# A patch-match network on one core: the first image is loaded over two queues ahead of the weights, and its first strips are gathered chunk by chunk

## The chip, the cores and the metric

The kernel runs on one core of one Trainium2 chip. The metric is the device time of one execution in microseconds (us), lower is better. The number compared is the median of several executions of the same program.

Engines, as the profile calls them: PE (matrix multiply; PEld is its weight load), DVE (vector), ACT (scalar/activation), POOL (GpSimd) and SP (SyncE, which here only issues DMAs). ACT and POOL issue DMAs too. Each engine takes its own instructions strictly in program order, so an instruction that waits holds back everything queued behind it on that engine.

## The reference

Eight images x[b] of 32 channels and 128 x 128 pixels go through two layers, each with a residual. Cut to what matters:

```python
n = group_norm(x)                                   # 16 groups
cost[o] = box3x3(sum_c (n - shift(n, o))**2)        # 25 offsets o of a 5x5 window
idx     = the 8 offsets with the lowest cost        # for every pixel
xb      = the 8 shifted copies of n picked by idx   # 32 * 8 = 256 channels
h = relu(dw2(w1 @ xb)); h = relu(dw4(w3 @ h))       # 1x1, then depthwise 3x3
wiener  = sigmoid(dw6(w5 @ h))
x = x + agg_w @ (inv_dct * (wiener * dct(xb)))
x = x + conv5x5(group_norm(x))                      # layer 1, one 5x5 kernel
```

## The kernel before

**Preparation of an image** (`prep`, L342). The image is loaded as `xn` with the four groups of 32 rows on the four quarters of the partitions (`load_image`, L78: one large DMA per quarter at L85, and six single edge rows at L90). Statistics (`bn_stats`, L349), a small matmul chain (`group_stats`, L254) and one scaling instruction (L360) normalise it. Then:

- `sources` (L375) transposes the rows and stores them to DRAM (`xl`, then `xtd`): 32 DMAs at L387 and 18 at L395/L399, all issued by POOL.
- `squares` (L403) forms the differences `df` on DVE (L414), their squares on ACT (L422), and the sum over channels on PE (L429, into `pd`). There are six groups of rows i = 0 to 5, with 12 differences each. `df` has four buffers, so DVE cannot write a fifth difference before PE has read the first. A finished group is copied (`sm`, L440) and stored to `sq` by POOL.
- After groups 1, 3, 4 and 5, `costs` (L455) of **chunk** 0, 1, 2 and 3 can run. A chunk is a quarter of the places: 8 of the 32 rows of every row group. 13 DMAs by POOL (L462, L469) bring the costs into `dsum`, DVE adds the 3 x 3 neighbours (`v`, L478 to L490, about four instructions), PE transposes (`pt`, L495), ACT copies (`ct`, L499), and DVE searches the eight best (L506, L507: 16 pairs for each half of a chunk).
- `places` (L512) turns a chunk's offsets into table places (`o`, L520 to L529, on DVE), PE transposes them, ACT casts them (`li`, L540), POOL stores them to DRAM (`idxd`, L541). Only then is the chunk marked `ready`.

**Gather** (units). An image has 16 strips of 8 rows; a strip has four units. `gather_load` (L552) has POOL load source pixels `xt` (three buffers) and two index tiles `ib` per unit by a DMA from `idxd` (L574; five buffers). `gather_select` (L582) makes a one-hot tile from each of them on ACT (L588, then L589). `gather_pixels` (L592) multiplies (`pg`, L603, PE) and ACT copies the result to `xb` (L610). Strip n needs chunk n % 4: strips 0 to 3 need one more chunk each, and from strip 4 on all chunks of that image are there.

**The three stages** of a strip, i = 1, 2, 3: `pointwise_v` (PE `pv` L641, ACT copy to `tv` L649), `pointwise_t` (PE `p` L665, ACT copy to `t` L672, and DMAs by SP), `depthwise_v` (ACT L692, then eight DVE multiply-adds `acc` at L695, ACT L699) and `depthwise_t` (PE `pw` L718, ACT L731). At the end `final_load`, `final_dct` (`pc` L777, DVE L785) and `final_add` (`pa` L798, DVE L805).

**The order** is written out by hand in the loop at L942: step s runs stage i on strip s - (i - 1) for i = 3, 2, 1 and then the final part, and in each of these four quarters it places one unit's gather: select of unit u + 1, load of unit u + 3, pixels of unit u. Preparation is made of generators in four queues ("D" with costs in us, "A", "P", "Q"); `tick` (L911) runs as much of "D" as is owed per quarter, and `until` (L918) runs the queues until a condition holds. `unit` (L892) calls `until` in front of a `gather_load` whose chunk is not yet `ready`, so that everything emitted later on PE, DVE and ACT stands behind that chunk's work. In `run` (L223) the first entry of "D" that is due is taken, except that at most two pairs of differences (cost `PAIR`) go between two runs of "Q".

Ahead of the loop, L932 loads units 0 to 6, selects up to unit 4 and gathers up to unit 3. As units 4 to 6 belong to strip 1, chunks 0 and 1 are both finished in front of strip 0's first stage, and the loads of the loop, three units ahead, ask for chunks 2 and 3 in the same way.

```python
        for u in range(7):
            unit(gather_load, u)
            unit(gather_select, u - 2)
            unit(gather_pixels, u - 3)
        u = 4
```

**Start.** The whole first image is issued by ACT (L95). SP meanwhile issues the constants `cst` (L97), the depthwise weights `dwv` and `dwt` (L123, L154), the pointwise weights (L174), 32 small DMAs `dq` (L284) and the rest. In the block at L148 the pointwise weights are reordered on DVE (`w_kc`, L179), transposed on PE (L189) and copied by ACT (L190); POOL builds `dwd` (L162) from `dwt`. `mixes` (L276) builds `ldct` and `lagg`.

Of the kernel before, what the change touches and what calls it, by code (L numbers as in the profile page):

```python
# [16 lines left out]
P = 128  # L17
C, K, H, W = 32, 8, 128, 128
CK = C * K
# [24 lines left out]
def bm3d_conv_preact(  # L44
# [30 lines left out]
        tc.tile_pool(name="ps_d", bufs=1, space=bass.MemoryType.PSUM)  # L75
    )

    def load_image(b, engine):  # L78

        xn = xnp.tile([P, HR, HX], F32, name=f"xn_{b}", tag="xn")  # L80
        for rg in range(4):
            s = slice(C * rg, C * (rg + 1))
            lo = 32 * rg - 3
            a, z = max(lo, 0), min(lo + HR, H)
            engine.dma_start(xn[s, a - lo : z - lo, 2 : 2 + W], x[b, :, a:z, :])  # L85
            for r in range(HR):
                y = lo + r
                if y < 0 or y >= H:
                    y = min(max(y, 0), H - 1)
                    engine.dma_start(  # L90
                        xn[s, r : r + 1, 2 : 2 + W], x[b, :, y : y + 1, :]
                    )
        return xn

    first = load_image(0, nc.scalar)  # L95
    cst = const.tile([P, C_N], F32, name="cst")
    nc.sync.dma_start(cst, consts)  # L97
    ident = cst[:, C_ID : C_ID + P]
# [46 lines left out]
    nc.vector.tensor_scalar(inner, inner, -1.0, 1.0, op0=ALU.mult, op1=ALU.add)  # L145


    with tc.tile_pool(name="setup", bufs=1) as sp, tc.tile_pool(  # L148
        name="setup_ps", bufs=2, space=bass.MemoryType.PSUM
    ) as spp:  # L150
        dwt = sp.tile([P, 3, 4, 9], F32, name="dwt")
        for n, w in enumerate((w2, w4, w6)):
            for g in range(4):
                nc.sync.dma_start(  # L154
                    dwt[C * g : C * (g + 1), n],
                    w[:P].rearrange("(q c) o a b -> c q (o a b)", c=C),
                )
            nc.gpsimd.memset(dwd[0:C, n, 1], 0.0)
            for u in range(2):
                for dy in range(3):  # L160
                    s = slice(C * (u + dy), C * (u + dy + 1))
                    nc.gpsimd.tensor_tensor(  # L162
                        dwd[s, n, u],
                        cst[s, C_M32 : C_M32 + C]
                        .unsqueeze(1)
                        .unsqueeze(1)
                        .to_broadcast([C, 4, 3, C]),
                        dwt[s, n, :, 3 * dy : 3 * dy + 3].unsqueeze(3).to_broadcast([C, 4, 3, C]),
                        ALU.mult,
                    )  # L170
        wide = {}
        for name, w in (("w1", w1), ("w3", w3), ("w5", w5)):
            t = sp.tile([P, 2, CK], F32, name=f"nat_{name}", tag=f"nat_{name}")
            nc.sync.dma_start(t, w.rearrange("(m p) i a b -> p m (i a b)", p=P))  # L174
            if name == "w1":

                nat, t = t, sp.tile([P, 2, CK], F32, name="w1_kc")
                for m in range(2):
                    nc.vector.tensor_copy(  # L179
                        t[:, m].rearrange("p (k c) -> p k c", c=C),  # L180
                        nat[:, m].rearrange("p (c k) -> p k c", k=K),
                    )
            wide[name] = t
        for name, dst in (("w1", lw1), ("w3", lw3), ("w5", lw5)):
            for g in range(2):
                ps = spp.tile([P, CK], F32, name=f"ps_{name}_{g}", tag="ps")
                for m in range(2):
                    src = wide[name][:, m, g * P : (g + 1) * P]
                    nc.tensor.transpose(ps[:, m * P : (m + 1) * P], src, ident)  # L189
                nc.scalar.copy(dst[:, g], ps)  # L190

    xbp = ctx.enter_context(tc.tile_pool(name="xb", bufs=2))
    accp = ctx.enter_context(tc.tile_pool(name="acc", bufs=1))
# [29 lines left out]
    def run(which, credit=1e9):  # L223

        q, took = queues[which], 0.0
        for _ in range(len(q) if which != "D" else 1000):

            i = next(
                (
                    i  # L230
                    for i, (c, _, at) in enumerate(q)
                    if at <= now[0] and (c != PAIR or pairs[0] < 2)
                ),
                None,
            )
            if i is None or took >= credit:
                break
            cost, task, _ = q[i]
            del q[i]
            took += cost  # L240
            pairs[0] += cost == PAIR
            push(task)
        if which == "Q":
            pairs[0] = 0
        return took
# [8 lines left out]
    def group_stats(mv, name):  # L254
# [18 lines left out]
        yield from inverse_std(mr[:, 1:2], tmp[:, 0:1], tmp[:, 0:1])  # L273
        return mr

    def mixes():  # L276

        dq = work.tile([P, 2, K], F32, name="dq", tag="dq", bufs=1)
        src = dct_w.rearrange("(m h c i) k a b -> m h k c (i a b)", m=2, h=2, i=K)
        for k in range(K):  # L280
            for m in range(2):
                for h in range(2):
                    p = 64 * h + 8 * k
                    nc.sync.dma_start(dq[p : p + 8, m], src[m, (h + m + 1) % 2, k])  # L284
        m8 = work.tile([P, 8], F32, name="m8", tag="m16", bufs=1)
        yield "D", 1.0
        nc.vector.tensor_reduce(
            m8,
            cst[:, C_M32 : C_M32 + C].rearrange("p (a c) -> p c a", c=8),
            axis=mybir.AxisListType.X,  # L290
            op=ALU.add,
        )
        for m in range(2):
            nc.vector.tensor_tensor(
                ldct[:, m].rearrange("p (c i) -> p c i", i=K),
                m8.unsqueeze(2).to_broadcast([P, 8, K]),
                dq[:, m].unsqueeze(1).to_broadcast([P, 8, K]),
                ALU.mult,
            )

        iv = work.tile([P, 2, K], F32, name="iv", tag="iv", bufs=1)
        nc.sync.dma_start(iv, inv_w.rearrange("(m p) k a b -> p m (k a b)", p=P))
        ag = work.tile([C, CK], F32, name="ag", tag="xr")
        nc.sync.dma_start(ag, agg_w.rearrange("c i a b -> c (i a b)"))
        for m in range(2):
            yield "D", 0.5
            ib = work.tile([P, P], F32, name=f"ib_{m}", tag="xm")
            nc.vector.tensor_tensor(
                ib.rearrange("p (c k) -> p c k", k=K),
                cst[:, C_M16 : C_M16 + 16].unsqueeze(2).to_broadcast([P, 16, K]),  # L310
                iv[:, m].unsqueeze(1).to_broadcast([P, 16, K]),
                ALU.mult,
            )
            yield "P", 0
            ps = ps_x.tile([P, 512], F32, name=f"ps_ag_{m}", tag="x")[:, :C]
            nc.tensor.transpose(ps, ag[:, m * P : (m + 1) * P], ident[:C, :C])
            agt = work.tile([P, C], F32, name=f"agt_{m}", tag="agt")
            nc.scalar.copy(agt, ps)
            yield "P", 0
            ps2 = ps_x.tile([P, 512], F32, name=f"ps_ia_{m}", tag="x")[:, :C]  # L320
            nc.tensor.matmul(ps2, ib, agt, start=True, stop=True)
            nc.scalar.copy(lagg[:, m], ps2)
# [602 lines left out]

    with tc.manual_schedule(engines=ORDERED):
        push(prep(0))
        push(mixes())
        xbd[0] = dram.tile([P, 2, H, W], F32, name="xbd_0", tag="xbd")
        for i in range(3):  # L930
            nc.gpsimd.memset(tb[i][0:64, :, 0], 0.0)
        for u in range(7):  # L932
            unit(gather_load, u)
            unit(gather_select, u - 2)
            unit(gather_pixels, u - 3)
        u = 4

        dt = dv = kept = iter(())

# [2 lines left out]
        for s in range(len(steps) + 2):  # L942
            if s < len(steps):
                b, n = steps[s]
                if s == 2:
                    push(bands())
                if n == (0 if b else 4) and b + 1 < NB:
                    until(lambda: b in ready, 4.0)
                    push(prep(b + 1))
                if n == NS - 1 and b + 1 < NB:  # L950
                    until(lambda: b + 1 in ready, 4.0)
                    xbd[b + 1] = dram.tile([P, 2, H, W], F32, name=f"xbd_{b+1}", tag="xbd")
            for i in (3, 2, 1, 0):
                si = s - (i - 1 if i else 2)
                live = 0 <= si < len(steps)
# [18 lines left out]
                    final_dct(bi, ni, accs[3, bi, ni], xf, j0, j1)  # L974

                run("Q")
                if s < len(steps):
                    unit(gather_select, u + 1, (0,))
                    unit(gather_load, u + 3)
                    tick(b, i)  # L980
                next(new_v, None)
                if live and i:
                    pointwise_t(i, bi, ni, lws[i - 1], src)
                next(kept, None)
                if s < len(steps):
                    unit(gather_pixels, u)
                next(dt, None)
                run("A")
                next(dv, None)
                if s < len(steps):  # L990
                    unit(gather_select, u + 1, (1,))
                    u += 1
                next(dt, None)
                kept, dv, dt = dv, new_v, new_t
                if live and not i:
# [68 lines left out]
```

## Time and profile before

| | us |
|---|---|
| median of 3 executions (lowest, highest) | 6942.3 (6939.84, 6943.18) |
| the profiled execution: its time, its span | 6939.75, 6938.0 |
| busy: PE, DVE, ACT, POOL | 6488.0, 5777.4, 5067.6, 3018.7 |
| first `bn_stats` of image 0 (L349) starts | 40.81 |
| first difference `df` (L414) starts | 52.85 |
| first `v` of chunk 0 (L478) starts | 95.52 |
| places of chunk 0, 1, 2, 3 ready on DVE (end of L529) | 134.49, 180.93, 229.75, 265.25 |
| step 4's first matmul (`pv`, L641, stage 3 of strip 2) starts | 382.77 |

Times inside the execution count from the start of the span. A group line of the profile gives the engine, what is written from what, how often, busy time and mean ns, then the idle time in front and what ended it. A line of the timeline gives start, length, engine, line, operation, and in brackets the idle time before it and its releaser. A line of the stretches view gives, for each engine, busy us and the number of instructions, and at its end the granted PE clock (1.00 is full), the busy share of the DMA engines and GB/s.

### The profile page before, as it was taken

The numbers are of one execution on the slowest core, as the hardware profiler recorded it, in microseconds if no ns is written. First come the engines' busy times: TensorE is split into PE (matmuls) and PEld (weight loads), VectorE is DVE, ScalarE is ACT, GpSimd is POOL, SyncE is SP. The second block draws the span as 40 slices with busy tenths as digits, with TensorE's granted clock in tenths as the row PEclk, the third lists the DMA queues.
The fourth block names the chain that finished last, engine by engine and source line by source line (L and its number), as shares of the span: only waits on it lengthen the run. The fifth ranks groups of instructions, "written<-read, shape, count | busy, mean of one in ns | idle before, by whom it ended". The sixth has DMA issues, their size and how long they took to land.

```text
span 6938.0 us, 230820 instructions
## 1 busy us (share of the span) xinstructions
PE 6488.0 (94%) x100450; PEld 3042.2 (44%) x100450; DVE 5777.4 (83%) x8606; ACT 5067.6 (73%) x6698; POOL 3018.7 (44%) x5143
## 2 busy tenths in 40 slices
PE   4699999999999999999999999999999999999997
PEld 1344444444444444444444444444444444444443
DVE  6689988889888898888988898888988889877775
ACT  4687778777687777877777776877768777776772
POOL 6345436334463344534445334553435433333332
PEclk9799999999999999999999999999999999999998
DMA  3566656557565575656756567565666666556652
GB/s 79 132 149 148 156 141 160 147 147 161 144 154 148 137 166 133 162 144 142 162 134 164 142 144 163 142 161 137 152 149 147 165 142 143 143 151 154 156 143 66
DMA packets 774196, 1007.83 MB, mean 145 GB/s; under 512 B 223712, under 2 KB 587168, under 8 KB 773184
## 3 DMA queue, kind: packets, MB, share of 16 engines
q0 software_dynamic: 387104, 733.70, 42.1%
q1 hardware_dynamic: 381056, 256.86, 17.2%
q8 instruction: 791, 12.96, 0.8%
q10 hardware_dynamic: 5024, 2.49, 0.2%
q14 instruction: 221, 1.81, 0.1%
HBM read 542.24 MB, written 217.01 MB: 109 GB/s over the span
## 4 chain that ended last, share of the span: by engine, by line
PE 48%; DVE 23%; issue 8%; DMA 8%; ACT 7%; POOL 5%; SPq 0%; POOLq 0%; DVEq 0%; ACTq 0%
PE pw L718 17%; DVE acc L695 16%; PE pv L641 12%; PE p L665 9%; PE pg L603 3%; PE p L861 3%; DMA t<-t 2%; DVE df L414 2%; PE pc L777 2%; DMA xf<-xbd 2%; DVE idx L507 2%; ACT ib L588 1%; PE pa L798 1%; ACT df L422 1%; DMA dsum<-sq 1%
## 5 line engine op out<-in xcount | busy, mean ns | idle before, releaser
L695 DVE SCALAR_TENSOR_TENSOR acc<-tv,dwv,acc 128x1024 f32<-128x1024 f32 (+3 forms) x3264 | 4031.9, 1237 | 242.1 <-ACT acc L692 126.5
L718 PE MATMUL pw<-t,dwd 96*32 96x508 f32 (+6 forms) x19392 | 2162.2, 592 | 84.7 <-DMA t<-t 58.5
L574 POOL DMA_DIRECT2D ib<-idxd x1024 | 566.7, 554 | 2185.9 <-ACT sel L589 2050.3
L718 PEld LDWEIGHTS pw<-t,dwd 96*32 96x32 f32 (+1 forms) x19392 | 712.3, 112 | 1216.7 <-issue 1135.5
L588 ACT ACTIVATE ib<-ib,nplace 128x1024 bf16<-128x1024 bf16 x1024 | 1170.6, 1143 | 19.1 <-DMA ib<-idxd 19.1
L589 ACT ACTIVATE sel<-ib 128x1024 f32<-128x1024 bf16 x1024 | 1084.5, 1059 | 32.5
L665 PE MATMUL p<-acc,lw 128*32 128x256 f32 x16768 | 981.7, 379 | 5.2 <-ACT tv L649 5.2
L641 PE MATMUL pv<-acc,lw 128*128 128x512 f32 (+1 forms) x2112 | 967.3, 601 | 16.7 <-DVE acc L785 16.0
L758 POOL DMA_DIRECT2D xf<-xbd x1088 | 648.7, 630 | 229.3 <-PE pc L777 121.3
L603 PE MATMUL pg<-sel,xt 128*32 128x48 f32 x45056 | 603.6, 209 | 151.3 <-DVE acc L785 63.7
L665 PEld LDWEIGHTS p<-acc,lw 128*32 128x32 f32 x16768 | 552.8, 111 | 427.2 <-issue 44.9
L649 ACT COPY tv<-pv 128x512 f32<-128x512 f32 (+2 forms) x784 | 438.8, 577 | 408.2 <-PE pv L641 399.4
L603 PEld LDWEIGHTS pg<-sel,xt 128*32 128x32 f32 x45056 | 586.6, 113 | 321.2 <-DVE acc L785 90.5
L422 ACT ACTIVATE df<-df 128x786 f32<-128x786 f32 (+2 forms) x576 | 468.8, 860 | 273.9 <-DVE df L414 271.1
L731 ACT ACTIVATE acc<-pw 128x512 f32<-128x512 f32 (+2 forms) x808 | 440.9, 572 | 268.6 <-PE pw L718 268.2
L641 PEld LDWEIGHTS pv<-acc,lw 128*128 128x128 f32 x2112 | 380.2, 191 | 505.7 <-issue 422.6
L672 ACT COPY t<-p 128x512 f32<-128x512 f32 x800 | 426.0, 571 | 225.1 <-PE p L665 223.0
L699 ACT ACTIVATE acc<-acc 128x1024 f32<-128x1024 f32 (+3 forms) x408 | 416.8, 1022 | 199.4 <-DVE acc L695 199.1
L805 DVE TENSOR_TENSOR xr<-xr,pa 128x256 f32<-128x256 f32 (+2 forms) x136 | 55.0, 404 | 587.3 <-PE pa L798 581.2
L414 DVE TENSOR_TENSOR df<-xn 128x786 f32<-128x786 f32 (+2 forms) x576 | 528.5, 967 | 11.4 <-PE pd L429 10.1
L692 ACT ACTIVATE acc<-tv,dwv 128x1024 f32<-128x1024 f32 (+3 forms) x408 | 454.6, 1114 | 51.7 <-PE pa L798 36.4
L641 PE MATMUL pv<-xb,lw 128*128 128x512 f32 x1024 | 474.3, 606 | 0.0
(128 smaller groups left out, 6041.6 us busy)
## 6 DMA issues: line engine op xcount, KB each, us to landing
ib<-idxd POOLq DMA_DIRECT2D x1024, 256.0 KB, 4.4
xbd<-xb POOLq DMA_DIRECT2D x128, 1024.0 KB, 6.4
xf<-xbd POOLq DMA_DIRECT2D x960, 128.0 KB, 6.6
t<-t SPq DMA_DIRECT2D x792, 128.0 KB
t<-t SPq DMA_DIRECT2D x384, 256.0 KB
tv<-tv SPq DMA_DIRECT2D x384, 130.0 KB
xt<-xtd POOLq DMA_DIRECT2D x240, 176.0 KB, 5.0
xl<-xs POOLq DMA_DIRECT2D x256, 64.0 KB, 2.3
```

Of the source, the lines that this page charges most:

```text
L414: nc.vector.tensor_sub(df[:, :, ca:cz], xn[:, r0 : r0 + SR, ca:cz], xn[:, r0 + dy : r0 + dy + SR, ca + dx : cz + dx],)
L422: nc.scalar.activation(df[:, :, ca:cz], df[:, :, ca:cz], AF.Square)
L574: nc.gpsimd.dma_start(ib.rearrange("p k y x -> p (k y x)"), idxd[b][s4 // 8, s4 % 8, 4 * k0 : 4 * k0 + 8] .rearrange("k x -> (k x)") .part ...
L588: nc.scalar.activation(ib, ib, AF.Square, bias=nplace)
L589: nc.scalar.activation(sel, ib, AF.Relu, scale=-1.0, bias=1.0)
L603: nc.tensor.matmul(pg[C * j : C * (j + 1), :, xa:xz], xt[:, t], sels[j // 2][:, j % 2, :, xa:xz], start=True, stop=True,)
L641: nc.tensor.matmul(ps[:, :hr], lhsT[:, g, P:CK], src(g)[:, h : h + hr], start=g == 0, stop=g == 1,)
L665: nc.tensor.matmul(ps[C * r : C * (r + 1), e, :nb], lhsT[:, g, s], rows[:, r : r + 4 * nb - 3 : 4], start=g == 0, stop=g == 1,)
L692: nc.scalar.activation(acc, rows, AF.Copy, scale=tap)
L695: nc.vector.scalar_tensor_tensor(acc, rows, tap, acc, op0=ALU.mult, op1=ALU.add)
L718: nc.tensor.matmul(pt[u][C * j : C * (j + 1), : nh[u], :nb, xa:xz], dwd[0:hi, i - 1, u, j, dx + 1], t[0:hi, j, : nh[u], :nb, xa + dx : xz ...
L758: nc.gpsimd.dma_start(xf[p : p + C, m, j0:j1], src[g, m, (h + m + 1) % 2, :, :, ya:yz])
```

## The change

1. `load_image` takes several engines and deals the four quarters of the image out in turn. Image 0 goes over ACT (quarters 0 and 2) and SP (quarters 1 and 3). SP issues its two quarters in front of `cst` and of all weights.
2. The load, reordering, transposing and copying of the pointwise weights leave the setup block and become a generator `weights()`, whose DVE, PE and ACT instructions are placed among the differences of image 0. Its tiles use `acc` buffers, its PSUM tiles come from the common pool. `mixes()` is due a little later too.
3. While image 0 has no chunks all ready (`0 not in ready`), `run("D")` takes any due entry that is not a pair of differences first. So the search and the places of a chunk come ahead of differences.
4. The units of strips 0 to 3 are gathered chunk by chunk: `begin(u)` loads three units and selects one, at the first unit of each chunk; `whole` places one unit complete, and nothing of the next chunk (`limit`). Strip 0's four units stand ahead of the loop. Step 0 gathers nothing. Steps 1 and 2 gather four units, two in each of their first two quarters; step 3 gathers eight, two in each quarter. From step 4 on it is one unit per quarter, as before.

The order of instructions that the changed kernel gives to PE is the same as before from its instruction row 679 on, which is step 4's first matmul, and it has the same PE instructions in all. DVE, ACT, POOL and SP, too, agree with before from about that point to the end.

```diff
-    def load_image(b, engine):
+    def load_image(b, *engines):
...
         for rg in range(4):
+            engine = engines[rg % len(engines)]
...
-    first = load_image(0, nc.scalar)
+    first = load_image(0, nc.scalar, nc.sync)
...
+            if which == "D" and 0 not in ready:
+
+                i = next((k for k, (c, _, at) in enumerate(q) if at <= now[0] and c != PAIR), i)
             if i is None or took >= credit:
...
+    def weights():
+
+        natural, kc = {}, None
+        for i, (name, w) in enumerate((("w1", w1), ("w3", w3), ("w5", w5))):
+            t = accp.tile([P, 2, R * W // 2], F32, name=f"nat_{name}", tag=f"acc{i + 1}0")
+            natural[name] = t = t[:, :, :CK]
+            nc.sync.dma_start(t, w.rearrange("(m p) i a b -> p m (i a b)", p=P))
+        yield "D", 1.0, 8
+
+        nat = natural["w1"]
+        kc = accp.tile([P, 2, R * W // 2], F32, name="w1_kc", tag="acc31")
+        natural["w1"] = kc = kc[:, :, :CK]
+        for m in range(2):
+            nc.vector.tensor_copy(
+                kc[:, m].rearrange("p (k c) -> p k c", c=C),
+                nat[:, m].rearrange("p (c k) -> p k c", k=K),
+            )
+        for name, dst in (("w1", lw1), ("w3", lw3), ("w5", lw5)):
+            for g in range(2):
+                yield "P", 0
+                ps = ps_x.tile([P, 512], F32, name=f"ps_{name}_{g}", tag="x")
+                for m in range(2):
+                    nc.tensor.transpose(
...
+                nc.scalar.copy(dst[:, g], ps[:, :CK])
...
-        yield "D", 1.0
+        yield "D", 1.0, 10
...
         push(prep(0))
+        push(weights())
         push(mixes())
...
-        for u in range(7):
-            unit(gather_load, u)
-            unit(gather_select, u - 2)
-            unit(gather_pixels, u - 3)
-        u = 4
+
+        def begin(u):
+            for k in range(3):
+                unit(gather_load, u + k)
+            unit(gather_select, u)
+
+        def whole(u, end):
+            if u + 1 < end:
+                unit(gather_select, u + 1)
+            if u + 3 < end:
+                unit(gather_load, u + 3)
+            unit(gather_pixels, u)
+            return u + 1
+
+        begin(0)
+        u = 0
+        while u < 4:
+            u = whole(u, 4)
...
+            count = {0: (0, 0, 0, 0), 1: (2, 2, 0, 0), 2: (2, 2, 0, 0), 3: (2, 2, 2, 2)}
+            count = count.get(s, (1, 1, 1, 1)) if s < len(steps) else (0, 0, 0, 0)
+            limit = 4 * (s + 1) if s < 3 else len(units)
+            if 0 < s < 4:
+                begin(u)
...
+                more = count[3 - i]
+                if more:
+                    if u + 1 < limit:
+                        unit(gather_select, u + 1, (0,))
+                    if u + 3 < limit:
+                        unit(gather_load, u + 3)
...
                     tick(b, i)
...
+                if more:
                     unit(gather_pixels, u)
...
+                if more:
+                    if u + 1 < limit:
+                        unit(gather_select, u + 1, (1,))
                     u += 1
+                    if more > 1:
+                        u = whole(u, limit)
```

More of the change, by code (lines that the diff above doesn't have):

```diff
@@ L145, in bm3d_conv_preact @@
     nc.vector.tensor_scalar(inner, inner, -1.0, 1.0, op0=ALU.mult, op1=ALU.add)
-    with tc.tile_pool(name="setup", bufs=1) as sp, tc.tile_pool(
-        name="setup_ps", bufs=2, space=bass.MemoryType.PSUM
-    ) as spp:
+    with tc.tile_pool(name="setup", bufs=1) as sp:
         dwt = sp.tile([P, 3, 4, 9], F32, name="dwt")
@@ L170, in bm3d_conv_preact @@
                     )
[L171 to L190, printed above, removed]
     xbp = ctx.enter_context(tc.tile_pool(name="xb", bufs=2))
@@ L274, in group_stats @@
         return mr
+    def weights():
[19 more added lines that the diff above has]
+                    nc.tensor.transpose(
+                        ps[:, m * P : (m + 1) * P],
+                        natural[name][:, m, g * P : (g + 1) * P],
+                        ident,
+                    )
+                nc.scalar.copy(dst[:, g], ps[:, :CK])
     def mixes():
@@ L976, in bm3d_conv_preact @@
                 run("Q")
+                more = count[3 - i]
[4 more added lines that the diff above has]
+                        unit(gather_load, u + 3)
                 if s < len(steps):
-                    unit(gather_select, u + 1, (0,))
-                    unit(gather_load, u + 3)
                     tick(b, i)
@@ L984, in bm3d_conv_preact @@
                 next(kept, None)
-                if s < len(steps):
+                if more:
                     unit(gather_pixels, u)
@@ L989, in bm3d_conv_preact @@
                 next(dv, None)
-                if s < len(steps):
-                    unit(gather_select, u + 1, (1,))
+                if more:
+                    if u + 1 < limit:
+                        unit(gather_select, u + 1, (1,))
                     u += 1
+                    if more > 1:
+                        u = whole(u, limit)
                 next(dt, None)
```

## The prediction

> **What bounds the kernel now.** I read the stretches view first, over the start of the execution, then the chain of waits, then the timeline of ACT and DVE. In the stretches the columns are PE, PEld, DVE, ACT, POOL, then PE clock, DMA share, GB/s.
>
> ```profile
> 52.85:95.50 42.65, 36.13 (x192) 9.85 (x192) 35.98 (x40) 36.21 (x51) 35.33 (x52) 1.00 0.34 64
> 95.50:134.50 39.00, 19.07 (x88) 4.34 (x88) 37.58 (x129) 18.48 (x24) 30.79 (x42) 0.82 0.46 100
> 134.50:181.00 46.50, 15.82 (x147) 5.24 (x147) 30.51 (x119) 20.62 (x26) 22.92 (x41) 0.72 0.28 75
> 181.00:230.00 49.00, 11.43 (x363) 9.71 (x364) 19.98 (x108) 22.14 (x26) 18.88 (x31) 0.53 0.44 111
> 340.00:382.80 42.80, 42.65 (x744) 20.30 (x742) 33.78 (x30) 34.08 (x43) 14.14 (x26) 1.00 0.66 149
> ```
>
> PE is full only from about 300 us on (42.65 of 42.80 us in the last row). Before that the start is held by DVE (37.58 of 39.00) or by nobody: from 134 to 230 us every engine is under two thirds. The page's 94% for PE says nothing of this stretch, and the change touches no other: from step 4's first matmul (382.77 us) all orders are the old ones. So the change is worth what it does to the time of that matmul. The chain of waits and DMA view show why the start begins late:
>
> ```profile
> 0.75 6.09 DMA xn<-in_x_dram
> 11.48 6.87 DMA xn<-in_x_dram
> 19.79 5.71 DMA dq<-in_L_conv_dct_w_dram
> 30.50 5.38 DMA dq<-in_L_conv_dct_w_dram
> 40.90 4.76 DVE st L349 x8
> ...
> q10 hardware_dynamic: 5024, 2.49, 22.3%
> ```
>
> The image's quarters alternate with SP's small DMAs. The last line (first 60 us; ACT's queue) says that the image itself needs 22.3% of 60 us, 13.4 us. The timeline shows the round trip of a chunk:
>
> ```profile
> 137.08 0.41 ACT L540 CAST li<-pi 128x128 bf16<-128x128 f32 x2
> 146.65 1.15 ACT L588 ACTIVATE ib<-ib,nplace 128x1024 bf16<-128x1024 bf16 x1 [9.16 <-DMA ib<-idxd]
> 201.42 1.15 ACT L588 ACTIVATE ib<-ib,nplace 128x1024 bf16<-128x1024 bf16 x1 [9.97 <-DMA ib<-idxd]
> 213.54 0.20 DVE L506 MAX8 mx<-ct 128x8 f32<-128x25 f32 x1 [25.25 <-ACT ct L499]
> ```
>
> From ACT's `li` over the store, the load and the landing of `ib` ACT stands still for 9 us, and DVE then waits for `ct` or squares that stand behind the selects in ACT's queue: 25.25 us here, 13.17 at 156.17. DVE's idle gaps from 95.5 to 382.8 add up to about 70 us.
>
> **The change, leg by leg.** F is the start of the first difference, before 52.85.
>
> *Leg 1, image.* `bn_stats` to first difference took 52.85 - 40.81 = 12.05 and stays. Two image queues bound the landing between 13.4 + 2 (first packets at about 2) = 15 and four quarters in turn at 6.1 to 6.9 plus edges, 28. No row shows two large loads side by side. `cst` now stands behind SP's half; it took 3.2 (0.76 to 3.98), and DVE needs it after two `bn_stats`: +1 to +3. F lies in 28 (15 + 12 + 1) to 43 (28 + 12 + 3); I take 31 (17 + 12 + 2), nearer the low end, as one queue fills the other's pauses (11.48 to 19.79 to 30.50 above): -21.9. Moved behind the image on SP: `dwt` ends about 23, so POOL's `dwd` (16.1) ends near 37; POOL's first `xl` is due at F + 5.3, so this is just hidden and costs up to 5 if not; between `xl` and `v` POOL has little to spare (35.33 busy of 42.65, and 2.2 of `xr` loads come in). `dq` (32 x 0.7) ends near 47, wanted by DVE at F + 21.
>
> *Leg 2, to the places of chunk 0.* Before 134.49 - 52.85 = 81.6. Up to `v`: 42.65 + 1.2, since four of the weights' ten ACT copies (0.40 and 0.17) come ahead of `sm` of group 1 on an ACT that is busy 36.21 of 42.65; the DVE part (2.9) and twelve transposes lie beside it; bounds 0 to 3.1. Then `v` 5.1, `pt` and `ct` 1.7, half a search 6.65, four differences 3.64, a wait for `ct` behind their squares 1.4, the other half 6.65, places 2.9: 71.9. Twelve differences fewer than before stand in between: -9.7.
>
> *Leg 3, to the places of chunk 1.* Before 46.4. Now ACT runs `li` at +1.15; `idxd` 1.6, four of the eight `xt` issues 1.95 (the other four go ahead), `ib` issue and landing 3.5 to 4: selects start at +8.5. **All eight** selects of strip 0 come first: 8 x 2.13 (pitch of a pair L588/L589) + copies and one wait for `pg` 3.4 = 20.5. Behind them in ACT's queue stand the squares of the last four differences of group 3; DVE, with four `df` buffers full, waits for one square and its matmul (1.7). DVE goes on at +31, having done 3.7: **idle 27**, where before it waited 13. Then DVE: 12 differences 11.1, strip 0's `acc` 10.5, `v` 5, search 13.3, 4 differences 3.7, places 2.9, waits 7.3 (pitch of PE and `ct`) = 53.8. Together 84.8: +38.4. The weights' tiles in `acc` buffers are read out long before the first `acc` (F + 114), which hides them; the PSUM pool that goes costs nothing for the same reason.
>
> *Leg 4, to chunk 2.* Before 48.8. Four differences and `v_2` take DVE 8.7; then it waits for `li` 1.2, round trip 7.7 (`ib` now waits for `idxd`, 2.45 as at 234.99), three selects 6.4, four squares 3.4, one select 2.1, `pg` 1.95, `pv` 4.2, one matmul 0.9, copies 0.6 = 28.4: **idle 19.7**. Then two differences 1.9, `acc` 10.5, a wait for `ct_2` behind selects and copies 6.5, `acc` 10.5, search 13.3, differences 1.8, bands 9, places 2.9: 56.4. Together 84.8: +36.0.
>
> *Leg 5, to chunk 3.* Before 35.5. Nothing is ready on DVE: `li` 1.2, round trip 9 (the next image's load stands between on POOL's queue, and its landing there took 6.5 at 194.87), two selects 4.3, copies 2.2: **idle 16.7**. Then three `acc` 31.6, `v_3` 5.3, search 13.3, L785 1.7, places 2.9, waits 1.3: 56.1. Together 72.8: +37.3.
>
> *Leg 6, to step 4.* Before 117.5, now `li` 1.2, round trip 7.8, then ACT without a pause: 16 selects up to the last gather 34.1, and 18.8 of copies and activations (3 x L692 at 1.1, 3 x L699 at 1.0, 6 `tv`, 6 `t`, 8 `xb` and 5 `pw` at about 0.5): 61.9. DVE's three `acc` (31.6) lie beside. -55.6.
>
> Sum: -21.9 - 9.7 + 38.4 + 36.0 + 37.3 - 55.6 = **+25** (24.5). Much the same from DVE: its work from `v` on is unchanged, `v` starts 20.7 earlier, and idle time grows from 70 to about 115.
>
> The profiled execution took 6939.75, 2.6 below the median of 6942.3; 6939.75 + 25 = 6964.8, so 6967 for the median.
>
> Bounds beside F: the waits of legs 3 to 6 were priced from rows with pitches known to 0.1, but the landing of `ib` showed 3.5 and 6.5: 4 x 3 = 12 up. PE's clock is 0.53 to 0.72 where it waits; 64 `p` took 6.10 at 266.06 and 3.59 at 276.70, and two such bursts are on DVE's waits: 0 to 5. After step 4 a later ACT (two selects behind) may cost or give 5.
>
> The Trainium skill, "TensorE: Matmul & The Clock Gate", Part 1, says that about 3.4 us of idleness halves PE's clock until it has worked as long. The trace agrees in sense (0.53 from 181 to 230 us); by the page each of the four waits would slow the next `pv` and `p`, and I would estimate +7 and a median of 6974; the rows alone give 6967. "DMA: Bandwidth & Descriptors", "Issuing engines are not separate DMA queues", says that a second issuing engine brings no bandwidth. Without that rule one would halve the 13.4, and the sum would be 6960; no row here shows two queues sharing.
>
> **Rivals.** (a) *The waits are no longer than before*: faster. The new order keeps ACT and DVE as overlapped as the lookahead did. For it: ACT is busy 215.66 of the 329.95 us from 52.85 to 382.8, so there is room for selects. Against: its queue is in order. The place is ACT in front of the first select of a chunk, the price 27 + 19.7 + 16.7 + 15.5 = 79 us of DVE idle; faster is decided if DVE's idle time from `v` on stays under about 90 - 14 = 76. With the old 70, Δ = -20.7: 6922. Chance 0.10. (b) *It cancels*: the waits are 20 to 30 shorter than I count: 6942. Chance 0.14. (c) *The two queues take turns*, F = 43: the image lands hardly sooner, as if that part did nothing: +37, 6979. Chance 0.21. My forecast: 0.55.
>
> **Numbers.** Differences under 0.2% (14 us) can't be told from no change. Forecast and (c) are slower, 0.76; (b) same 0.14; (a) faster 0.10. The range: F = 28 with shorter waits, +22 - 10, up to F = 43 with late landings, +37 + 9: 6954 to 6988; lowered to 6940 to take in part of (b).
>
> **What would show it.** In the changed profile: first difference near 31; places 0, 1, 2, 3 done near 103, 188, 273, 345; step 4's first `pv` at 407. ACT waits for `ib` from DMA four times, 7 to 9 us each, in place of two. DVE idles about 27 us behind the eight selects. I am wrong if places 1 come before 175, if step 4 starts before 383, or if the time after step 4 differs from before's 6555 by more than 5.

## The result and the profile after

The changed kernel is slower: 6970.5 us median (6957.9 to 6977.3, 6 executions) against 6941.1 (6938.0 to 6947.4, 6 executions) of the kernel before on the same chip. The ratio is 1.0041, 95% interval 1.0028 to 1.0053. The forecast was 6967 in a range of 6940 to 6988.

The profiled execution took 6957.9, the lowest of its six, with a span of 6956.0. The stretches of the start, cut where the places of a chunk are about to come (columns as before: PE, PEld, DVE, ACT, POOL, then PE clock, DMA share, GB/s):

```profile
30.00:75.00 45.00, 39.26 (x208) 11.62 (x210) 42.00 (x48) 38.35 (x61) 43.92 (x58) 1.00 0.32 60
75.00:110.00 35.00, 7.37 (x30) 2.63 (x28) 26.51 (x116) 4.78 (x8) 28.67 (x37) 0.63 0.47 101
110.00:185.00 75.00, 38.95 (x560) 17.51 (x560) 39.25 (x103) 41.79 (x52) 35.25 (x62) 0.68 0.35 91
185.00:270.00 85.00, 39.70 (x634) 19.92 (x634) 57.95 (x177) 37.56 (x49) 19.89 (x34) 0.70 0.28 73
270.00:340.00 70.00, 50.78 (x738) 24.51 (x738) 45.97 (x91) 36.35 (x48) 18.28 (x31) 0.81 0.53 123
```

Two things are to be seen. In the first row POOL is full (43.92 of 45.00 us), which it was not before (35.33 of 42.65). In the third no engine reaches 42 of 75 us: here the first of the lost time lies (the rest follows in front of chunks 2 and 3, as the table of legs further below shows). The timeline of ACT shows the round trip of chunk 0 and the order behind it, that of DVE what it costs:

```profile
107.56 0.48 ACT L551 CAST li<-pi 128x128 bf16<-128x128 f32 x2 [10.22 <-PE pi L549]
115.36 1.15 ACT L599 ACTIVATE ib<-ib,nplace 128x1024 bf16<-128x1024 bf16 x1 [7.32 <-DMA ib<-idxd]
...
132.39 1.06 ACT L600 ACTIVATE sel<-ib 128x1024 f32<-128x1024 bf16 x1
133.36 0.57 ACT L621 COPY xb<-pg 128x512 f32<-128x512 f32 x1
135.47 0.58 ACT L621 COPY xb<-pg 128x512 f32<-128x512 f32 x1 [1.55 <-PE pg L614]
135.95 2.35 ACT L433 ACTIVATE df<-df 128x786 f32<-128x786 f32 x3
```

```profile
138.51 3.65 DVE L425 TENSOR_TENSOR df<-xn 128x792 f32<-128x792 f32 x4 [27.97 <-PE pd L440]
```

ACT waits 7.3 us for `ib`, runs eight selects (115.36 to 133.4), and only then the squares (L433) that PE and so DVE wait for. DVE stands still for 28 us. From the first `v` to step 4's first matmul, DVE's work is the same as before (212.7 and 212.8 us), and all that grows is its idle time, the length of the stretch less its busy time, from 74.5 to 121.0 us:

```profile
95.52:382.77 287.25, 188.01 (x3056) 89.02 (x3056) 212.74 (x569) 179.45 (x227) 120.91 (x197) 0.82 0.50 123
```

```profile
78.93:412.74 333.81, 189.22 (x3057) 93.06 (x3057) 212.83 (x569) 174.39 (x223) 120.09 (x195) 0.74 0.41 103
```

In the table of waits ACT's wait for `ib` is now four times, in place of 19.1 us in two:

```profile
ACT ib L599 <- DMA ib<-idxd: 32.8, 4, 11.2
```

The image, in the chain of waits and the DMA view, is no longer cut into pieces:

```profile
0.75 8.96 DMA xn<-in_x_dram
10.08 6.44 DMA xn<-in_x_dram
```

It has landed when `bn_stats` starts at 16.50 (before 40.81), and the first difference F starts at 30.14 (before 52.85). Step 4's first matmul:

```profile
412.74 3.70 PE L652 MATMUL pv<-acc,lw 128*128 128x512 f32 x8
```

That is 30.0 later than before (382.77), and the medians differ by 29.4.

### The profile page after: what moved, and what is told of

It is laid out like the page before. It is cut to its first block, busy times and chain, and to the rows that moved or that the text cites. A ratio compares the mean times of both kernels' runs of the same rounds, so it can differ in the third digit from the quotient of the medians.

```text
span 6956.0 us, 230798 instructions
## 1 busy us (share of the span) xinstructions
PE 6479.5 (93%) x100450; PEld 3034.3 (44%) x100450; DVE 5780.9 (83%) x8606; ACT 5064.6 (73%) x6698; POOL 3026.0 (44%) x5143
## 4 chain that ended last, share of the span: by engine, by line
PE 51%; DVE 20%; ACT 9%; issue 8%; DMA 7%; POOL 4%; SPq 0%; DVEq 0%; ACTq 0%; POOLq 0%
PE pw L729 17%; DVE acc L706 13%; PE pv L652 13%; PE p L676 10%; PE pg L614 4%; PE p L872 3%; DMA t<-t 3%; ACT ib L599 2%; DVE df L425 2%; PE pc L788 2%; DMA xf<-xbd 1%; PE pa L809 1%; ACT df L433 1%; DVE idx L518 1%; ACT acc L703 1%
## 5 line engine op out<-in xcount | busy, mean ns | idle before, releaser
L599 ACT ACTIVATE ib<-ib,nplace 128x1024 bf16<-128x1024 bf16 x1024 | 1170.4, 1143 | 32.8 <-DMA ib<-idxd 32.8
L433 ACT ACTIVATE df<-df 128x786 f32<-128x786 f32 (+2 forms) x576 | 467.7, 861 | 289.5 <-DVE df L425 287.0
```

What stands on the lines that cost most here:

```text
L433: nc.scalar.activation(df[:, :, ca:cz], df[:, :, ca:cz], AF.Square)
L599: nc.scalar.activation(ib, ib, AF.Square, bias=nplace)
```

## The experiments

My theory: the image and the weights alone make the kernel faster by some 20 us; gathering chunk by chunk costs more than that, in two parts: ACT's round trip over DRAM, which comes four times, and the order in ACT's queue, where selects stand in front of squares. Rival: the loss comes from places ahead of differences (part 3), or from POOL at the start.

All ratios are to the kernel before on the same chip, with 95% intervals; the rest is from each kernel's profiled execution, in us. DVE's idle time is counted from the stretches view, as above.

| kernel | ratio | F | v of chunk 0 | places 0, 1, 3 | step 4 | DVE idle from v on |
|---|---|---|---|---|---|---|
| before | | 52.9 | 95.5 | 134.5, 180.9, 265.3 | 382.8 | 75 |
| changed | 1.0041 (1.0028–1.0053) | 30.1 | 78.9 | 107.0, 191.1, 350.1 | 412.7 | 121 |
| e1 parts 1, 2 | 0.9973 (0.9964–0.9982) | 30.5 | 79.3 | 118.3, 164.7, 250.4 | 362.2 | 70 |
| e2 parts 1, 2, 3 | 0.9976 (0.9966–0.9986) | 30.0 | 78.7 | 106.8, 169.3, 248.7 | 360.4 | 69 |
| e3 part 4 | 1.0047 (1.0034–1.0060) | 53.2 | 95.1 | 134.1, 203.1, 350.5 | 413.2 | 105 |
| e4 parts 1, 2, 4 | 1.0022 (1.0012–1.0033) | 30.1 | 78.8 | 117.8, 187.3, 334.8 | 397.6 | 106 |
| e5 squares between | 1.0005 (0.9996–1.0014) | 30.4 | 79.1 | 107.2, 171.5, 319.5 | 381.9 | 90 |
| e7 no round trip | 1.0017 (1.0009–1.0026) | 33.6 | 84.3 | 112.4, 188.5, 330.9 | 387.9 | 91 |
| e11 no `dwd` | 1.0050 (1.0037–1.0063) | 29.2 | 73.9 | 102.0, 185.9, 344.9 | 407.9 | 121 |
| e12 parts 1, 2, `dwd` held | 0.9982 (0.9973–0.9990) | 29.0 | 74.6 | 113.6, 163.1, 248.1 | 361.8 | 72 |

**Which part does it: e1 to e4.** e1 is the kernel before with the image over two queues and `weights()`; gather and `run` are the old ones. Its difference to the changed kernel:

```diff
-            if which == "D" and 0 not in ready:
-                i = next((k for k, (c, _, at) in enumerate(q) if at <= now[0] and c != PAIR), i)
...
-        begin(0)
-        u = 0
-        while u < 4:
-            u = whole(u, 4)
+        for u in range(7):
+            unit(gather_load, u)
+            unit(gather_select, u - 2)
+            unit(gather_pixels, u - 3)
+        u = 4
```

> Before with parts 1 and 2 of the change alone: image 0 over two queues, the weights among the differences; the search order and the gather order stay as before. Theory (the loss is the chunk-by-chunk gather): first difference near 30, v of chunk 0 near 79 as in the changed kernel, so 16.6 earlier than before, and the rest as before: 6941 - 17 = 6924, in 6914 to 6932. Rival (the weights among the differences, or SP's late small loads, cost the time): near the changed kernel, 6960 or more.

It is faster by 0.27%, and step 4 comes 20.6 earlier: nearly all of the 22.3 by which F comes earlier. Parts 1 and 2 were not run one without the other. e2 is e1 with the two lines of `run` put back:

```diff
+            if which == "D" and 0 not in ready:
+                i = next((k for k, (c, _, at) in enumerate(q) if at <= now[0] and c != PAIR), i)
```

> Parts 1, 2 and 3: as the run before, and places and searches ahead of differences, still with the old gather order of seven loads and three units of lookahead. Theory: the total of DVE's work is unchanged and strip 0 needs chunks 0 and 1 as before, so within 12 of the run with parts 1 and 2 alone, 6924. Rival (taking places first starves ACT and PE of squares and costs the time): 6950 or more.

Chunk 0 is 11 us sooner, but chunk 1 4.6 later, and the time is the same. With the old gather, part 3 is neutral. e3 is the kernel before with part 4 alone (`begin`, `whole`, and in the loop `count` and `limit`, as in the diff of the change):

```diff
-        for u in range(7):
-            unit(gather_load, u)
-            unit(gather_select, u - 2)
-            unit(gather_pixels, u - 3)
-        u = 4
+        begin(0)
+        u = 0
+        while u < 4:
+            u = whole(u, 4)
...
+            if 0 < s < 4:
+                begin(u)
```

> Before with part 4 alone: units of strips 0 to 3 gathered chunk by chunk, image and weights and search order as before. Theory: the four round trips through ACT's queue are exposed without any gain at the start: ACT waits four times 7 to 11 us for ib, DVE idles 20 or more behind strip 0's eight selects, step 4 starts 25 to 45 later than 382.8, and the time is 6966 to 6986. Rival (the gather order is neutral): 6941.

Part 4 costs 30.4 us at step 4 without any other part, 0.47% in the median. e4 is the changed kernel without part 3:

```diff
-            if which == "D" and 0 not in ready:
-                i = next((k for k, (c, _, at) in enumerate(q) if at <= now[0] and c != PAIR), i)
```

> The changed kernel without part 3: pairs of differences lie among the searches again. Theory: part 4's waits stay, but the differences are made beside the searches instead of after them, so that less stands behind the selects: e3 less 17, 6950 to 6968. Rival (taking places first is what costs): 6925 to 6940.

Step 4 comes 14.9 later than before and 15.1 sooner than with part 3. So part 3, neutral in e2, costs 15 us beside part 4: with it chunk 0's places end 10.8 sooner and chunk 1's 3.8 later, and DVE idles 15 more: 3 in front of chunk 0's places, 7.5 in front of chunk 1's and 9 in front of chunk 3's, against 4.5 less in front of chunk 2's. In front of chunk 1's the likely reason is that the differences which it passes are left over behind the eight selects; in front of chunk 3's ACT's wait for `ib` is 11.2 in place of 6.7. No run isolates either.

**What makes part 4 dear: e5 and e7.** e5 runs the preparation's queues between the units of strip 0, so that squares come between selects in ACT's queue. The same lines also bring chunk 1's costs and the differences forward in DVE's and PE's order; nothing else in the program changes.

```diff
         while u < 4:
+            for _ in range(2):
+                now[0] += 1
+                run("D", 4.0)
+                run("A")
+                run("P")
+                run("Q")
             u = whole(u, 4)
```

> The changed kernel, but between strip 0's units the queues of preparation are run (two rounds, at most 4 us of D each), so that differences and their squares of groups 3 to 5 and the costs of chunk 1 stand between strip 0's eight selects in ACT's and DVE's order. The work is the same. Theory (the selects at the head of ACT's queue hold DVE back, not the amount of work): DVE's gap of 28.0 before 138.5 shrinks to 12 or less, places of chunk 1 come 15 to 20 earlier than 191.1, step 4 starts near 395 and the time is 13 to 20 below the changed kernel, ratio 1.0013 to 1.0023. Rival (DVE waits for the landing of ib whatever the order): gap and time stay within 5, ratio 1.0041.

ACT's timeline in e5, after the same wait for `ib` as before:

```profile
115.42 1.15 ACT L599 ACTIVATE ib<-ib,nplace 128x1024 bf16<-128x1024 bf16 x1 [7.20 <-DMA ib<-idxd]
...
119.69 3.08 ACT L433 ACTIVATE df<-df 128x786 f32<-128x786 f32 x4
124.39 0.49 ACT L451 COPY sm<-pd 128x396 f32<-128x396 f32 x1 [1.61 <-PE pd L440]
124.77 3.11 ACT L433 ACTIVATE df<-df 128x792 f32<-128x792 f32 x4
```

```profile
122.23 1.88 DVE L425 TENSOR_TENSOR df<-xn 128x792 f32<-128x792 f32 x2 [11.52 <-PE pd L440]
```

The squares start 16 us sooner, DVE's gap is 11.5 in place of 28.0, and step 4 comes 30.8 sooner, level with before. This is more than the gap (16.5) gives: the second chunk's wait for `ib` is gone too and later gaps are shorter (DVE idles 31 less in all). It is also more than I had expected (step 4 near 395, a ratio of at least 1.0013). Mixing the two kinds of work is worth the whole loss of the changed kernel against before; at step 4 e5 is still 21.6 behind e2, which has the old gather.

e7 takes the round trip away instead: the index tiles of image 0's strips 0 to 3 come from a DRAM tile filled with zeros at the start, so their pixels don't depend on the search.

```diff
-                idxd[b][s4 // 8, s4 % 8, 4 * k0 : 4 * k0 + 8]
+                (idxd[b] if b or s4 > 7 else other)[s4 // 8, s4 % 8, 4 * k0 : 4 * k0 + 8]
```

> The changed kernel, but the index tiles ib of strips 0 to 3 of image 0 are loaded from a DRAM tile of zeros that is written at the start, not from the places of their chunk: it leaves out the dependence of those four strips on the search (all their places are 0), and the store, load and landing of ib are no longer waited for. All instructions keep their order. Theory: ACT's four waits for ib (7.3, 7.1, 11.2, 7.2: 32.8) go; sel starts right behind li; of them some 25 to 33 are gained, step 4 starts at 380 to 390, ratio 0.9995 to 1.0008. Rival (only the order in ACT's queue costs, the round trip is covered): step 4 stays within 8 of 412.7.

```profile
112.92 0.48 ACT L558 CAST li<-pi 128x128 bf16<-128x128 f32 x2 [10.21 <-PE pi L556]
113.30 1.15 ACT L606 ACTIVATE ib<-ib,nplace 128x1024 bf16<-128x1024 bf16 x1
```

No wait stands between the two. The stores of the zeros made F 3.4 and `v` 5.4 later, so I compare from `v` on: 303.6 to step 4 against 333.8, 30.2 less, close to the 32.8 of the four waits. The ratio of 1.0017 missed the expected 0.9995 to 1.0008: the late start leaves step 4 5.2 behind before, and the median is 12 behind; no run explains the rest. DVE's gap behind the eight selects is still 20.6. So both causes are real, each with about 30 us when taken away alone. Whether they add up is open: both together were not tried. In full is unlikely, since 30.8 and 30.2 are together more than the 52.4 by which the changed kernel's step 4 comes behind that of e2.

**Leg 2's 5 us: e6 and e9 to e12.** `v` started at F + 48.8 where I had summed F + 43.9. POOL's and DVE's timelines in the changed kernel:

```profile
18.13 21.86 POOL L161 TENSOR_TENSOR dwd<-cst,dwt 32x384 f32<-32x384 f32 x18 [10.25 <-DMA dwt<-in_L_conv_w_dram]
39.94 3.15 POOL L398 DMA_DIRECT2D xl<-xs  x4
```

```profile
30.14 15.11 DVE L425 TENSOR_TENSOR df<-xn 128x792 f32<-128x792 f32 x12
```

The 18 multiplies took 21.86 (16.11 before) and the first twelve differences 1.26 each on average, not 0.9. One multiply ran beside the scaling of `xn` on DVE and took 3.27 in place of under 0.9, and the last six, beside the differences, 9.13 together:

```profile
26.80 3.31 DVE L371 TENSOR_SCALAR xn<-xn,mr_a 128x5016 f32<-128x5016 f32 x1
```

```profile
27.54 3.27 POOL L161 TENSOR_TENSOR dwd<-cst,dwt 32x384 f32<-32x384 f32 x1
30.86 9.13 POOL L161 TENSOR_TENSOR dwd<-cst,dwt 32x384 f32<-32x384 f32 x6
```

e6 lets `cst` go out first on ACT and POOL load `dwt`, to have `dwd` done before F.

```diff
-    first = load_image(0, nc.scalar, nc.sync)
...
-    nc.sync.dma_start(cst, consts)
+    nc.scalar.dma_start(cst, consts)
+    first = load_image(0, nc.scalar, nc.sync)
...
-                nc.sync.dma_start(
+                nc.gpsimd.dma_start(
```

> The changed kernel with the depthwise weights dwt loaded by POOL and the constants first on ACT, so that POOL's 18 dwd multiplies end before the first difference. Theory of the 5 us missed in leg 2 (POOL's dwd and DVE's first differences slow each other: dwd 21.86 instead of 16.11, twelve differences 15.11 instead of 11): dwd takes 16 again, twelve differences 11 to 11.5, v of chunk 0 comes 4 to 6 earlier after the first difference than 48.8, and the time is about 5 below the changed kernel, ratio 1.0034. Rival (the differences are slow because PE's clock or ACT is slow at the start, POOL only issues late): twelve differences still take 15.

It failed in its means (1.0062, 1.0049 to 1.0075; `v` at F + 49.4, step 4 at 413.9): POOL's own DMA issues came between the multiplies, and six of them still ran beside the first differences, five without a break:

```profile
20.99 4.41 POOL L161 TENSOR_TENSOR dwd<-cst,dwt 32x384 f32<-32x384 f32 x5
...
32.11 7.34 POOL L161 TENSOR_TENSOR dwd<-cst,dwt 32x384 f32<-32x384 f32 x5
...
40.91 5.31 POOL L398 DMA_DIRECT2D xl<-xs  x7
```

The rows show the slowing all the same: five multiplies took 4.41 before F and 7.34 beside differences. e8 is e1 with the same edit, and came out like e1: 0.9980 (0.9972 to 0.9989), step 4 at 362.0.

> Parts 1 and 2 alone (e1) with the dwd edit of e6, as the version that should beat both kernels. Theory: e1's 0.9973 less 5 us, 0.9966; first difference near 30, v near 74, step 4's start near 357. Rival (in e1's order POOL is not the limit): 0.9973.

e9 and e10 put the multiplies later in the text of the changed kernel and of e1 (six for each stage; `spread(n)` holds what stood in the loop over the weights):

```diff
+        spread(0)
...
+                if s in (1, 2):
+                    spread(s)
```

> The changed kernel, with POOL's 18 multiplies of dwd moved from the start of its queue to the places where their weights are first wanted: six behind strip 0's gather, six at step 1, six at step 2. What the multiplies write is the same. Theory A (on POOL and DVE at the start): leg 2 came out 5 us longer than I summed because the 18 multiplies run beside the first differences; both slow down, xl is issued only at 39.9, and POOL then has no slack up to v. With them gone, the twelve first differences take 11 to 12 us in place of 15.1, xl is issued by 35 to 37, v of chunk 0 starts at F + 43 to F + 45 in place of F + 48.8, and step 4's first matmul comes 3 to 6 us sooner: 407 to 410, median ratio to the kernel before 1.0033 to 1.0038. Theory B: v is bound by ACT (four copies of weights ahead of sm) or by the landing of the small DMAs, not by POOL; v stays at F + 48 to F + 49 and nothing is gained. If six multiplies at a later place hold POOL's index stores or xt loads, a new gap of 5 us shows there and eats the gain.

> The kernel with the image over two queues and the weights among the differences (parts 1 and 2 alone, old gather and old order of differences), with POOL's 18 multiplies of dwd moved to behind the gather of strip 0's first unit, to the end of the opening gather and to step 1, six each. Theory A (POOL and DVE slow each other at the start and POOL has no slack up to v): v of chunk 0 at F + 43 to F + 45 in place of F + 48.7, step 4's first matmul at 356 to 359 in place of 362.2, median ratio to the kernel before 0.9963 to 0.9970 where parts 1 and 2 alone gave 0.9973. Theory B (v bound by ACT or by DMA landings): v at F + 48 to F + 49 and the same time as parts 1 and 2 alone.

The multiplies did not move: the order written out by hand binds PE, DVE and ACT but not POOL, and in both traces all 18 ran from 18.2 or 18.5 for 21.9 us. So the two test neither theory, and count as repeats of their parents: 1.0057 (1.0043 to 1.0071) and 0.9980 (0.9971 to 0.9990), step 4 at 415.0 and 366.9. They show that step 4 itself varies by 2 to 5 us between kernels with nearly the same order. (e11's expectation says that seven multiplies ran from 28.0 to 40.4; that was the part of the 18 that the view's window showed.)

e11 leaves the multiplies out:

```diff
-                    nc.gpsimd.tensor_tensor(
-                        dwd[s, n, u],
...
+    nc.gpsimd.memset(dwd, 0.02)
```

> The changed kernel without POOL's 18 multiplies: dwd is filled with one constant by a single memset at the start, so the depthwise 3x3 weights of 128 of each layer's channels are not those of the reference; every other instruction stays. The attempt to move the multiplies by their place in the program did not move them (seven of them still ran from 28.0 to 40.4, beside the first differences), so here they are gone. Theory A: they and DVE's first differences slow each other and hold back xl; without them the twelve first differences take 11 to 12 us (15.1 with them), xl is first issued between F + 2 and F + 6, v of chunk 0 starts at F + 43 to F + 46 (F + 48.8 with them), step 4's first matmul at 407 to 410 (412.7). Theory B: v is bound by ACT or by the landings of small DMAs behind; F + 48 to F + 49.

```profile
29.19 7.22 DVE L413 TENSOR_TENSOR df<-xn 128x792 f32<-128x792 f32 x8
36.62 3.63 DVE L413 TENSOR_TENSOR df<-xn 128x786 f32<-128x786 f32 x4 [0.21 <-PE pd L428]
...
73.94 1.11 DVE L477 TENSOR_TENSOR v<-dsum 128x910 f32<-128x910 f32 x1 [5.41 <-DMA xl<-xs]
```

```profile
34.51 3.12 POOL L386 DMA_DIRECT2D xl<-xs  x4 [25.73 <-ACT xs L384]
```

The first twelve differences take 0.9 each, `xl` goes out at F + 5.3, as soon as ACT has copied it, and `v` starts at F + 44.8, where the other kernels with the new image load and the 18 multiplies from about 18 on (changed, e1, e2, e4, e5, e9, e10) have F + 48.7 to F + 48.8. Theory A is shown for `v`. Step 4 comes 4.9 sooner, at 407.9, about as much as step 4 differs between e1 and its repeat e10 (4.7). The median doesn't show these 5 us: its ratio of 1.0050 has an interval of ±0.13%, or 9 us.

e12 is e1 with the multiplies held back by data: they read a copy of `dwt` to which zero times a place of chunk 0 is added.

```diff
+            nc.gpsimd.tensor_scalar(late, o[:, 0:1], 0.0, None, op0=ALU.mult)
+            nc.gpsimd.tensor_scalar(dwt2, dwt, late, None, op0=ALU.add)
```

> Parts 1 and 2 of the change alone (image over two queues, weights among the differences, old gather), with the 18 multiplies of dwd held back until the places of chunk 0 are there: they read a copy of the weights to which POOL adds zero times a place of chunk 0. What is computed is the reference's. Theory A: v of chunk 0 at F + 43 to F + 46 (F + 48.7 without the hold), step 4's first matmul at 356 to 360 (362.2), ratio to the kernel before 0.9963 to 0.9972 (0.9973). Theory B: v at F + 48 to F + 49, step 4's first matmul at 362 or later. If the multiplies, now between the loads of indices, hold back POOL's loads of chunk 0, the second unit's selects are late by up to 16 us and the gain is lost there.

`v` starts at F + 45.6 and chunk 0's places end 4.7 sooner than in e1, but step 4 only 0.4 sooner. The multiplies now run beside the differences that lie among chunk 1's searches, and these slow down in their turn. The multiplies, two of the differences in e1, and the four pairs in e12:

```profile
136.54 12.89 POOL L163 TENSOR_TENSOR dwd<-cst,dwt 32x384 f32<-32x384 f32 x10
```

```profile
141.70 1.84 DVE L422 TENSOR_TENSOR df<-xn 128x780 f32<-128x780 f32 x2
```

```profile
137.63 2.99 DVE L424 TENSOR_TENSOR df<-xn 128x780 f32<-128x780 f32 x2
142.19 2.48 DVE L424 TENSOR_TENSOR df<-xn 128x780 f32<-128x780 f32 x2
146.25 2.48 DVE L424 TENSOR_TENSOR df<-xn 128x786 f32<-128x786 f32 x2
150.31 1.84 DVE L424 TENSOR_TENSOR df<-xn 128x786 f32<-128x786 f32 x2
```

The last pair, behind the end of the multiplies, takes 1.84 again; the other three have lost 2.4 together. By chunk 1's places 1.6 of the 4.7 are left. My third case put the loss at the second unit's selects; most of it came from DVE. The fastest versions that I have are those without part 4 (e1, e2, e8, e10, e12, ratios 0.9973 to 0.9982); their intervals overlap.

## Why the prediction was right

Direction, mechanism and size held: 29.4 us in the median against 25, and the time in the range. Leg by leg, in the profiled execution:

| | predicted | measured |
|---|---|---|
| leg 1, first difference F | 31 | 30.1 |
| leg 2, F to places of chunk 0 | 71.9 | 76.9 |
| leg 3, to chunk 1 | 84.8 | 84.1 |
| leg 4, to chunk 2 | 84.8 | 82.3 |
| leg 5, to chunk 3 | 72.8 | 76.7 |
| leg 6, to step 4 | 61.9 | 62.7 |
| step 4 | 407 | 412.7 |

*Leg 1* held, and for the reason given: `bn_stats` starts at 16.5 where I took 17, and it is followed by the same chain. I had written that no row shows two large loads side by side, or two queues sharing. One does: before, SP's three loads of 256 KB for the pointwise weights were issued while ACT's second quarter began (11.48), and the DMA view at the end has 194 to 255 GB/s for both together in slices 12 to 16.

```profile
11.02 1.54 SPq L174 DMA_DIRECT2D nat_w<-in_L_conv_w_dram  x3
```

*Leg 2* is the term that was mis-sized, by 5.0. That this is nearly the whole difference of 5.5 at step 4 is in part luck, since legs 4 and 5 missed by -2.5 and +3.9 and cancel in part. I wrote that `dwd` "ends near 37", is "just hidden and costs up to 5 if not", and priced it at 16.1 from a stretch in which DVE did almost nothing (3.24 us of the first 25). It ended at 39.99, since it ran beside the scaling of `xn` and the differences, and POOL, without slack, carried the delay to `v`. e11 gives F + 44.8 without it, 0.9 from my 43.9. The Trainium skill would have told: "SBUF — State Buffer", "Who interferes with whom", says that a DVE instruction with two inputs in SBUF contends with a GpSimd instruction that reads SBUF. The same page, "SBUF: two separate sides", says that whichever starts first keeps the shared ports for the whole instruction. The traces agree in sense: alone a difference took 0.9 and a multiply 0.88 (e12, 3.52 for four); beside each other six multiplies took 1.52 each (the row of 9.13). That lies between 0.9 and the 1.8 (my estimate, 0.9 + 0.88) of strict turns, so strict turns are not shown.

*Leg 3*: the gap behind the eight selects was predicted at 27 and is 28.0; e5, with other work between them, shrinks it to 11.5. *Leg 4*: idle 19.7 predicted, 18.7 measured. *Leg 5* took 3.9 more: ACT waited 11.2 for `ib` where I counted 9, since this load took 6.8 us (278.78 in the chain of waits), a little above the upper of the two landings that I had named as a bound. That is 2.2 of the 3.9.

```profile
278.78 6.81 DMA ib<-idxd
```

*Leg 6*: ACT's work of 61.9 without a pause came out at 62.7.

Idle time of DVE was to grow by 45 (from 70 to 115) and grew by 46.5. The stretches view gives 74.5 and 121.0; the 70 of the prediction was a sum of gaps and is 4.5 lower. Four waits for `ib` of 7 to 9 us are 7.3, 7.1, 11.2 and 7.2.

The clock: by the Trainium skill, "TensorE: Matmul & The Clock Gate", Part 1, I had estimated +7. Legs 3 to 6 sum to 305.7 against 304.3 from the rows without it, and the clock is 0.68 and 0.70 from 110 to 270 where before had 0.72 and 0.53 from 134.5 to 230. No run here shows the surplus; none was made to separate it.

One sign that I had set was wrong. The time after step 4 is 6543.2, 12 less than before's 6555.2, where I allowed 5. But from there on the orders are the old ones, and over the profiled executions of all these kernels that time lies anywhere from 6536.9 (e9) to 6557.7 (e4), with no relation to the edit. The sign was too tight for one execution; the medians agree with step 4.

The rivals: (a), "the waits are no longer than before", would need DVE's idle time under 76, or about 80 as the stretches view counts it; it is 121. Its number, -20.7 at step 4 with the old idle time, is what e1 shows where the gather stays as it was (-20.6, idle 70). (b), waits 20 to 30 shorter, is what the order of e5 makes (idle 90, ratio 1.0005). (c), the two queues take turns, F = 43, fell: F is 30.1.

## What to carry to other kernels

Work that comes early is worth nothing if what it releases is put, whole, in front of the work that another engine waits for: on an engine that takes its queue in order, count what stands behind the inserted block and who waits for that (eight selects here, 28 us of DVE), and mix the two instead (e5, 31 us at step 4). Try the parts of a change one by one: here two of four parts gain 0.27%, and the other two turned that into a loss of 0.41%. A duration taken from a row holds only with the neighbours that the row had; look at who ran beside it before moving it.

## What was not expected of the hardware

DVE's two-input differences and POOL's multiplies slow each other: 0.9 and 0.88 us alone, 1.26 on average over the first twelve differences, 1.52 over the six multiplies beside them. The scaling of `xn` at 26.80 took 3.31 in place of 2.89 (before, and in e6, where no multiply ran beside it), and the multiply beside it 3.27 in place of under 0.9: it ended 0.7 after the scaling.

The image landed 24 us sooner with hardly more bandwidth: the transfers were paused before, not slow. The DMA view of the first 45 us, 40 slices each, of before and then of after:

```profile
GB/s 0 60 269 230 165 37 1 16 32 23 33 249 255 194 253 201 77 0 58 253 172 72 1 18 35 21 0 5 170 218 118 0 0 1 29 44 14 5 0 0
```

```profile
GB/s 0 47 210 196 178 181 176 176 212 204 188 187 181 201 115 8 9 9 11 8 77 324 291 13 0 0 1 0 1 0 0 1 0 1 0 1 55 63 117 59
```

While they flow, the old transfers are as fast (253 GB/s in slice 20, where the image has the DMA engines to itself) as the new (176 to 212 from slice 3 to 14). The difference is in when the issues came. Before, ACT issued its second, third and fourth quarter from 11.48 on, and this took 19.13 us; after, both engines had issued both their quarters by 3.6 us:

```profile
0.75 0.43 ACTq L85 DMA_DIRECT2D xn<-in_x_dram  x1
7.94 2.42 ACTq L90 DMA_DIRECT2D xn<-in_x_dram  x3
11.48 19.13 ACTq L85 DMA_DIRECT2D xn<-in_x_dram  x3
```

```profile
0.75 0.43 ACTq L86 DMA_DIRECT2D xn<-in_x_dram  x1
1.21 1.80 ACTq L91 DMA_DIRECT2D xn<-in_x_dram  x3
3.04 0.52 ACTq L86 DMA_DIRECT2D xn<-in_x_dram  x1
```

How much of this is the second queue, and how much that SP's small loads now stand behind the image, no run separates. What holds an issue back on a queue with a large load in front was not tried by itself either: three of ACT's four came late here, and in the changed kernel SP's edge rows behind its two quarters took 8.50 us.
